# Masking the second attention step by a comparison instead of a match-and-replace pass

## The chip, the cores and the metric

The kernel runs on one core of one Trainium2 chip. The metric is the device time of one launch in microseconds (us). Five engines work side by side, each with its own in-order queue of instructions: TensorE (PE) multiplies matrices and transposes, VectorE (DVE) and ScalarE (ACT) do element-wise work and reductions, GpSimd (POOL) issues the indirect gathers and a few additions, and SyncE (SP) issues most of the plain transfers. On-chip memory is SBUF (128 partitions) and PSUM, where matmul results land; HBM holds the arrays and what is stored in between.

## The reference, cut to what matters

Two graph layers follow each other on 3327 nodes with 256 features. The first has two steps; each builds a 3327 x 3327 attention matrix, keeps in each row the largest probabilities that together reach 90% of the row's mass, and scales the rest of the row to sum 1:

```python
def _top_p_attention(X, W1, W2, W3):
    q = X @ W1.T @ W2.T
    k = X @ W3.T
    probs = softmax(q @ k.T, axis=-1)
    idx = argsort(-probs, axis=-1)
    sp = take_along_axis(probs, idx, axis=-1)
    keep_sorted = cumsum(sp, axis=-1) - sp < 0.9
    mask = zeros(probs.shape, bool).at[rows, idx].set(keep_sorted)
    A = probs * mask
    return A / maximum(A.sum(-1, keepdims=True), 1e-12)

R = row_normalised(adj + I)
for n in range(2):                 # step 0, step 1
    A = _top_p_attention(Xa, W1, W2, W3)
    Xf = R @ Xf
    Xa = A @ Xa
    Z = Z + Xf @ U1[n].T + Xa @ U2[n].T
layer_0 = layernorm(X + Z)         # added to x
# layer 1: relu(D^-1/2 adj D^-1/2 h W.T + b), added to x
```

The sort is stable: of several equal values at the cut only as many are kept as the mass needs.

## The kernel before

The 3327 nodes are tiled into `NB` = 26 blocks of 128 rows. A block of an attention step holds a strip `e` of 128 x 3327 values exp(logit) in SBUF (three such strips, tag "e"). The work has these stages: a start that normalises x and makes keys and queries; step 0 over 26 blocks, mixed with the listing of the sparse adjacency and its gathered products; step 1 over 26 blocks, mixed with the second adjacency product and the layer norms; and a late stage with the second layer (gathered or dense adjacency products, output matmul, store).

**One block of attention** (`attention`, L1321) is a set of named pieces. `lg`/`ex`: PE makes the logits `p_l`, ACT turns them into `e` with a row sum z. `guess`, `ev1r`, `ev1s`, `st1`, in step 1 also `mass`, `tail`, `ev2s`, `btw1`, `sec1`: ACT passes over `e` (written to `ja`, L927) and short 128 x 1 operations on ACT and DVE close in on a threshold t a little above the cut. `win` (L1049): DVE copies the values up to t into a strip `w` of the same size, with their sum. `wm`: 16 MAX8 operations (L1056) take the 8 largest of each of 16 windows of `w`. `sort` (L1060 to L1069): five MAX8 with match-and-replace between them sort out the 40 largest, `val`. `cut` (`window_cut`, L1071): a prefix sum of `val` starts from the mass above t; a value is dropped where its prefix has reached 90% of z (`out_` is then -1e30, otherwise 0), and `kept8` (L1092) receives the eight smallest kept values of each row, the smallest first.

**The mask** differs between the steps. In step 0, a further `cut6` counts ties: `tied` (L1095) is the sum of `out_` over the values of `val` that are at least the smallest kept one, so it is 0 without and at most -1e30 with a dropped value equal to it. `drop` (`drop_rest`, L1111, operation at L1114) then keeps `e >= kept8[0]` and sums the kept into `den`. In step 1, `match` (`mark_kept`, L1105, operation at L1109) first copies `e` to `w` and replaces one entry for each of the eight values of `kept8` by 1e30; `drop` keeps the entries whose `w` is greater than `kept8[0]`. So of equal values only as many are kept as `kept8` lists.

After the mask come the groups of PE transposes `tr` (`p_t`, L1128, two PSUM buffers), ACT copies `atc` (`at`, L1134) and matmuls `att` (`att_acc`, L1143), four blocks of 128 at a time. In step 1, `block_1` (L1436) then makes the residual and norms (`resid`, `input2`), `node2` writes the next layer's input `hn` (ACT, L1284, with a `shift` from DVE, L1283), and `stn` stores it.

**Order.** Nothing is scheduled at run time. `plan_block` (L1473) gives each piece of block i the time BASE + PERIOD * i + SHIFT + place, with the places written out in the table `PLACES`, and `Plan.run` emits the pieces in the order of these times. This order is the order within each engine's queue; `in_steps` (L278) splits a helper at its yields into pieces such as cut0 to cut6.

**The checks.** After the last piece the flags `good` (L1723 to L1741) collect for each row and step whether the 40 values sufficed, whether the cut lies inside them, and whether ties could have gone wrong: for step 0 from `tied`, for step 1 from `kept8[0] < kept8[7]`. One bad row makes the branch at L1746 run `network_bits` (L1663), which computes everything again with a bisection over the bits of the threshold (`nucleus_bits`, L1612: 27 passes over the strip and one more for each of 52 blocks).

Of the kernel before, what the change touches and what calls it, by code (L numbers as in the profile page):

```python
# [10 lines left out]
F32 = mybir.dt.float32  # L11
# [3 lines left out]
ALU = mybir.AluOpType  # L15
AX = mybir.AxisListType

P = 128
N = 3327
NB = (N + P - 1) // P  # L20
# [43 lines left out]
BIG = 1e30  # L64
FILL = 8
# [70 lines left out]
        btw1=-17.852, st14=-15.208, aux0=-14.988, aux1=-14.22, sec10=-12.922, sec11=-12.131, sec12=-10.743,  # L136
        thr=-7.89, sec13=-7.788, nt2=-2.992, win=2.783, wm2=6.046, wm0=6.444, wm1=6.454, wm3=6.526, sort0=8.121,
        sort1=8.162, sort2=9.437, sort3=10.527, sort4=11.217, sort5=12.023, sort6=12.773, sort7=13.564, sort8=15.249,
        cut0=15.328, sort9=15.348, cut1=16.458, cut2=17.341, cut3=18.102, cut4=18.886, cut5=19.961, match=21.123,
        drop=23.999, tr0=28.827, atc0=29.172, tr4=29.605, tr1=32.779, att0=32.801, tr2=32.803, atc1=33.007,  # L140
        att1=33.809, atc4=34.739, tr3=34.759, atc2=36.727, att2=37.933, tr5=38.539, tr6=39.45, atc3=40.18,
        att3=40.29, ldx=44.319, atc5=45.361, atc6=45.991, ldh=48.128, att4=48.571, inv=49.727, att5=50.339,
# [135 lines left out]
def in_steps(do, name, n, work):  # L278
    steps = iter(())

    def step():
        nonlocal steps
        if not started:
            steps = work()
            started.append(True)
        next(steps, None)

    started = []
    do.update((f"{name}{k}", step) for k in range(n))
# [19 lines left out]
def tile_kernel(ctx: ExitStack, tc: tile.TileContext, x, adj_t, w1t, w2t, w3t, u1t, u2t, ln_g, ln_b, wt, bias, out):  # L309
    nc = tc.nc  # L310
    nc.scalar.preload_act_table_set("natural_log_exp_and_others")

    const = ctx.enter_context(tc.tile_pool(name="const", bufs=1))
    res = ctx.enter_context(tc.tile_pool(name="res", bufs=1))
    big = ctx.enter_context(tc.tile_pool(name="big", bufs=1))
    work = ctx.enter_context(tc.tile_pool(name="work", bufs=2))
    small = ctx.enter_context(tc.tile_pool(name="small", bufs=3))
# [92 lines left out]
    kept8 = const.tile([P, 2 * NB, 8], F32, name="kept8")  # L410
# [9 lines left out]
    listed = const.tile([P, NB], F32, name="listed")  # L420
    crowd = const.tile([P, NB], F32, name="crowd")
    edge = const.tile([P, 2 * NB], F32, name="edge")
    tied = const.tile([P, NB], F32, name="tied")
    hidden = const.tile([P, 2 * NB], F32, name="hidden")

    def inv_sqrt(dst, src, eps):
# [375 lines left out]
    def query_load(step, s, i):  # L802
        s["q"] = work.tile([P, P], F32, name="q", bufs=3)
        for half in range(2):
            nc.sync.dma_start(s["q"][half * DA : (half + 1) * DA], q_hbm[step][i * DA : (i + 1) * DA])
# [52 lines left out]
    def logit_group(s, kt, g):  # L858

        c0, w = LOGIT_GROUPS[g]  # L860
        s["l", g] = pl = ps_l.tile([P, 2 * GROUP_W], F32, tag="psl", name="p_l")
        for c in range(0, w, LOGIT_W):
            cw = min(LOGIT_W, w - c)
            for half in range(2):
                rows, at = slice(half * DA, (half + 1) * DA), half * GROUP_W + c
                nc.tensor.matmul(  # L866
                    pl[:, at : at + cw], s["q"][rows, :], kt[rows, c0 + c : c0 + c + cw], start=True, stop=True
                )
# [7 lines left out]
    def exp_group(s, g):  # L876

        c0, w = LOGIT_GROUPS[g]
        if "e" not in s:
            s["e"] = big.tile([P, N + FILL], F32, tag="e", name="e", bufs=3)  # L880
            s["zp"] = z_free[0]
            z_free.append(z_free.pop(0))
        nc.scalar.activation(  # L883
            halves(s["e"])[:, :, c0 : c0 + w], logits_of(s.pop(("l", g)))[:, :, :w], AF.Exp,
            accum_out=s["zp"][:, g : g + 1],
        )

    def col(name):
        return small.tile([P, 1], F32, name=name)
# [39 lines left out]
    def eval_over_by_vector(s):  # L929

        junk = big.tile([P, N + FILL], F32, tag="w", name="w_over")[:, :N]
        s["over"] = col("over")
        ev = s["e"][:, :N]
        nc.vector.scalar_tensor_tensor(
            junk, ev, s["t"], ev, op0=ALU.max, op1=ALU.subtract, accum_out=s["over"]
        )
# [134 lines left out]
    def window_cut(i, step, s):  # L1071


        at, depth = step * NB + i, DEPTH
        s["pre"] = pre = small.tile([P, DEPTH + 1], F32, name="pre", bufs=3)
        nc.vector.tensor_sub(pre[:, 0:1], s["z"], s["below"])
        yield
        val = s.pop("val")
        nc.vector.tensor_tensor_scan(
            pre[:, 1 : depth + 1], val[:, :depth], val[:, :depth], initial=pre[:, 0:1], op0=ALU.add, op1=ALU.bypass  # L1080
        )
        yield
        out_ = small.tile([P, DEPTH], F32, name="out_", bufs=2)
        nc.vector.tensor_scalar(out_[:, :depth], pre[:, :depth], s["thr"], -BIG, op0=ALU.is_ge, op1=ALU.mult)
        yield
        neg = small.tile([P, DEPTH], F32, name="neg", bufs=2)
        nc.vector.tensor_sub(neg[:, :depth], out_[:, :depth], val[:, :depth])
        yield
        neg8 = small.tile([P, 8], F32, name="neg8")
        nc.vector.max(neg8, neg[:, :depth])  # L1090
        yield
        nc.vector.tensor_scalar_mul(kept8[:, at, :], neg8, -1.0)  # L1092
        if step == 0:
            yield
            nc.vector.scalar_tensor_tensor(  # L1095
                out_[:, :depth], val[:, :depth], kept8[:, at, 0:1], out_[:, :depth], op0=ALU.is_ge, op1=ALU.mult,
                accum_out=tied[:, i : i + 1],
            )

    def window_edge(i, step, s):  # L1100

        at = step * NB + i
        nc.vector.tensor_tensor(edge[:, at : at + 1], s.pop("pre")[:, DEPTH - 1 : DEPTH], s["thr"], op=ALU.subtract)

    def mark_kept(i, step, s):  # L1105


        s["w"] = big.tile([P, N + FILL], F32, tag="w", name="w")
        nc.vector.match_replace(s["w"], kept8[:, step * NB + i, :], s["e"], BIG)  # L1109

    def drop_rest(i, step, s):  # L1111
        den, ev = col("den"), s["e"][:, :N]
        kept, op = (ev, ALU.is_ge) if step == 0 else (s.pop("w")[:, :N], ALU.is_gt)
        nc.vector.scalar_tensor_tensor(  # L1114
            ev, kept, kept8[:, step * NB + i, 0:1], ev, op0=op, op1=ALU.mult, accum_out=den
        )
        s["den"] = den

# [202 lines left out]
    def attention(step, i, s, kt, v):  # L1321

        do = {}
        s.update(at={})
        do["ldq"] = lambda: query_load(step, s, i)
        for n in range(NZ):
            do[f"lg{n}"] = lambda n=n: logit_group(s, kt, n)
            do[f"ex{n}"] = lambda n=n: exp_group(s, n)
        in_steps(do, "guess", 7 if step else 9, lambda: first_guess(s, step))
        by_vector = i < BY_VECTOR[step]  # L1330
        do["ev1r"] = lambda: eval_over_by_vector(s) if by_vector else eval_pass(s, AF.Relu, "over")
        do["ev1s"] = lambda: eval_pass(s, AF.Sign, "sign")
        do["thr"] = lambda: set_thr(step, s)
        if step == 0:
            in_steps(do, "st1", 9, lambda: step_0(s))
        else:
            in_steps(do, "mass", 3, lambda: prepare_mass(s))
            do["half"] = lambda: prepare_half(s)
            in_steps(do, "tail", 4, lambda: tail_slope(s))
            in_steps(do, "st1", 5, lambda: step_1(s))  # L1340
            do["aux0"] = lambda: prepare_size(s)
            do["aux1"] = lambda: prepare_num(s)
            do["aux2"] = lambda: prepare_goal(s)
            do["ev2s"] = do["ev1s"]
            do["btw1"] = lambda: count_between(s)
            in_steps(do, "sec1", 4, lambda: secant(s))
            do["nt2"] = lambda: last_t(s)
        do["win"] = lambda: window(s)
        for n in range(4):
            do[f"wm{n}"] = lambda n=n: [window_max(s, k) for k in range(4 * n, 4 * n + 4)]  # L1350
        in_steps(do, "sort", 10, lambda: window_sort(i, step, s))
        in_steps(do, "cut", 6 if step else 7, lambda: window_cut(i, step, s))
        do["edge"] = lambda: window_edge(i, step, s)
        if step == 1:
            do["match"] = lambda: mark_kept(i, step, s)
        do["drop"] = lambda: drop_rest(i, step, s)
        do["inv"] = lambda: invert(s)
        for g in range(GROUPS):
            do[f"tr{g}"] = lambda g=g: attend_turn(s, g)
            do[f"atc{g}"] = lambda g=g: attend_copy(s, g)  # L1360
            do[f"att{g}"] = lambda g=g: attend_sum(s, g, v)
        return do
# [359 lines left out]

    good = small.tile([P, 2 * NB], F32, name="good", bufs=1)  # L1723
    nc.vector.tensor_tensor(good, hidden, kept8[:, :, 0], op=ALU.is_lt)
    also = small.tile([P, 2 * NB], F32, name="also", bufs=1)
    nc.vector.scalar_tensor_tensor(good, edge, 0.0, good, op0=ALU.is_ge, op1=ALU.mult)
    nc.vector.scalar_tensor_tensor(good, kept8[:, :, 0], BIG / 2, good, op0=ALU.is_lt, op1=ALU.mult)
    nc.vector.tensor_tensor(also, kept8[:, :, 0], kept8[:, :, 7], op=ALU.is_lt)
    nc.vector.tensor_scalar(also[:, :NB], tied, -1.0, None, op0=ALU.is_ge)
    nc.vector.tensor_mul(good, good, also)  # L1730
    for c in range(LAST, P):
        for s in range(2):
            g = good[:, (s + 1) * NB - 1 : (s + 1) * NB]
# [54 lines left out]
```

## Time and profile before

| | us |
|---|---|
| three timed runs | 1647.74, 1652.57, 1652.86 |
| their median | 1652.57 |
| the profiled execution | 1856.47 |
| its span, first to last instruction | 1854.7 |
| DVE, PE, ACT, POOL busy in the span | 1301.9, 1543.8, 1139.2, 1004.3 |
| step 0, about | 90 to 930 |
| step 1, about | 965 to 1608 |
| late stage | 1608 to 1855 |

All durations below come from the one profiled execution, which took longer than the timed runs. The page gives busy time by engine, the span in 40 slices of 46.4 us with a digit for tenths of busy time, the groups of instructions by line and operation (busy us, mean ns of one, idle time of the engine just before them and what ended it), and the chain of work that ended last. A row "engine line waited for <- what" sums the idle time of an engine before that line's instructions by what ended it. Matmul ends are modelled and matmuls overlap, so a busy PE isn't a PE at its peak.

### The profile page before, as it was taken

The page shows a single profiled execution, that of the slowest core. Times are in us where ns is not written, and L with a number is a line of the kernel's source. Part 1 is how long each engine was busy: PE and PEld are TensorE (multiplying, and loading weights), DVE is VectorE, ACT ScalarE, POOL GpSimd, SP SyncE. Part 2 cuts the span into 40 slices and gives each one's busy share as a digit, 9 for nine tenths or more (in the row PEclk, how much of TensorE's full clock was granted, in tenths as well). Part 3 has the DMA queues.
Part 4 walks back from the last instruction along what each step waited for, and adds up shares of the span by engine and source line. Part 5 has one row for each costly group of instructions (what it writes and reads, how often), then busy time and mean ns, then how long its engine had stood idle before and what let it go on. Part 6 is the DMA issues. An engine that isn't in the chain of part 4 may idle for free.

```text
span 1854.7 us, 24872 instructions
## 1 busy us (share of the span) xinstructions
PE 1543.8 (83%) x7372; PEld 1191.4 (64%) x7372; DVE 1301.9 (70%) x3965; ACT 1139.2 (61%) x2692; POOL 1004.3 (54%) x808
## 2 busy tenths in 40 slices
PE   5957698878977788787867999999999998968786
PEld 3535476756765566666645777777777777757675
DVE  5596577856865677676629999999999999301111
ACT  3564566645664565666468999999999995100000
POOL 0076465767456456675535665365566461256663
PEclk9968799988988999898987999999999999989998
DMA  6555566645534555453443343333344442647643
GB/s 187 172 170 178 156 178 197 198 133 169 175 120 123 181 147 165 154 172 89 125 145 119 115 121 120 109 116 110 109 118 124 136 120 79 206 142 244 201 142 107
DMA packets 149167, 272.26 MB, mean 147 GB/s; under 512 B 29603, under 2 KB 94496, under 8 KB 148000
## 3 DMA queue, kind: packets, MB, share of 16 engines
q1 hardware_dynamic: 109456, 181.58, 30.2%
q0 software_dynamic: 33536, 87.08, 17.0%
q10 hardware_dynamic: 6032, 1.93, 0.5%
q8 instruction: 60, 0.98, 0.2%
q14 instruction: 83, 0.68, 0.1%
HBM read 221.08 MB, written 49.41 MB: 146 GB/s over the span
## 4 chain that ended last, share of the span: by engine, by line
DVE 22%; PE 13%; issue 11%; another core or an unknown queue 5%; ACT 4%; DMA 1%; POOL 1%; SPq 0%; DVEq 0%; ACTq 0%; POOLq 0%
DVE cand L1056 6%; DVE w L1109 5%; PE att_acc L1143 3%; PE late_acc L702 2%; PE late_sums L1554 2%; ACT ja L927 2%; PE p_t L1128 1%; DVE cand L1069 1%; DVE val L1066 1%; PE adj_acc L702 1%; PE p_o L1299 1%; PE p_l L866 1%; DVE e L1114 1%; DVE bn_st L442 1%
## 5 line engine op out<-in xcount | busy, mean ns | idle before, releaser
L692 POOL DMA_INDIRECT vg<-y_hbm,v_idx x208 | 327.7, 1576 | 273.3 <-PE adj_acc L702 184.1
L678 POOL DMA_INDIRECT ac<-in_adj_t,a_idx x208 | 264.6, 1272 | 253.1 <-DVE own L619 84.7
L1143 PE MATMUL att_acc<-h,at 128*128 128x256 f32 (+1 forms) x1352 | 353.0, 406 | 54.5 <-issue 30.3
L927 ACT ACTIVATE ja<-e,t 128x3327 uint8<-128x3327 f32 x127 | 389.6, 3068 | 0.7
L1134 ACT COPY at<-p_t 128x512 f32<-128x512 f32 (+1 forms) x364 | 197.6, 547 | 238.4 <-remote 123.4
L1143 PEld LDWEIGHTS att_acc<-h,at 128*128 128x128 f32 (+1 forms) x1352 | 266.5, 204 | 111.8 <-issue 43.6
L692 POOL DMA_INDIRECT vg<-gb_hbm,v_idx x208 | 247.6, 1190 | 135.8 <-PE adj_acc L702 72.2
L1143 PE MATMUL att_acc<-xa,at 128*128 128x256 f32 (+1 forms) x1352 | 321.0, 382 | 0.0
L1128 PE MATMUL p_t<-ident,e 128*128 128x128 f32 x1352 | 216.3, 287 | 83.7 <-DVE e L1114 38.3
L1143 PEld LDWEIGHTS att_acc<-xa,at 128*128 128x128 f32 (+1 forms) x1352 | 252.4, 192 | 31.4
L1128 PEld LDWEIGHTS p_t<-ident,e 128*128 128x128 f32 x1352 | 166.7, 147 | 144.3 <-issue 39.4
L1056 DVE MAX8 cand<-w 128x8 f32<-128x208 f32 x832 | 238.6, 360 | 0.2
L702 PE MATMUL adj_acc<-vg,ac 128*128 128x257 f32 (+1 forms) x832 | 229.3, 388 | 2.5 <-issue 1.3
L866 PE MATMUL p_l<-kt,q 64*128 64x512 f32 (+1 forms) x832 | 194.7, 577 | 35.0 <-ACT e L883 27.6
L1049 DVE SCALAR_TENSOR_TENSOR w<-e,t 128x3327 f32<-128x3327 f32 x52 | 191.2, 3676 | 41.5 <-ACT t L897 17.9
L692 POOL DMA_INDIRECT vg<-hn_hbm,v_idx x144 | 136.9, 950 | 97.0 <-PE late_acc L702 48.2
L883 ACT ACTIVATE e<-p_l 128x2048 f32<-128x2048 f32 x104 | 161.6, 1554 | 34.4 <-remote 10.1
L702 PEld LDWEIGHTS adj_acc<-vg,ac 128*128 128x128 f32 x832 | 149.2, 192 | 27.5 <-issue 7.0
L866 PEld LDWEIGHTS p_l<-kt,q 64*128 64x128 f32 x832 | 78.5, 199 | 124.4 <-issue 80.6
L730 ACT COPY xt_k<-p_turn 128x256 f32<-128x256 f32 x52 | 19.0, 370 | 177.9 <-PE late_acc L702 78.6
L570 DVE TENSOR_REDUCE most<-adj_sb 128x7 f32<-128x896 f32 x104 | 105.2, 1012 | 2.0 <-DMA adj_sb<-in_adj_t 1.1
L1114 DVE SCALAR_TENSOR_TENSOR e<-e,kept 128x3327 f32<-128x3327 f32 x26 | 95.7, 3680 | 2.1 <-DVE kept L1092 1.7
(397 smaller groups left out, 2128.6 us busy)
## 6 DMA issues: line engine op xcount, KB each, us to landing
ac<-ac_hbm SPq DMA_DIRECT2D x70, 512.0 KB
adj_sb<-in_adj_t SPq DMA_DIRECT2D x78, 448.0 KB
ac_hbm<-ac SPq DMA_DIRECT2D x26, 512.0 KB
adj_row<-in_adj_t SPq DMA_DIRECT2D x8, 1664.0 KB
adj_sb<-in_adj_t SPq DMA_DIRECT2D x26, 320.0 KB
gb_hbm<-gb SPq DMA_DIRECT2D x26, 256.0 KB
gb<-gb_hbm SPq DMA_DIRECT2D x26, 256.0 KB
q<-q_hbm SPq DMA_DIRECT2D x104, 32.0 KB
```

Of the source, the lines that this page charges most:

```text
L678: nc.gpsimd.indirect_dma_start(s["list"][:, k, :], None, adj_rows, bass.IndirectOffsetOnAxis(ap=s["a_idx"][:, k : k + 1], axis=0))
L692: nc.gpsimd.indirect_dma_start(t[:, :D], None, hbm[:, :], bass.IndirectOffsetOnAxis(ap=v_idx[:, i, k : k + 1], axis=0))
L702: nc.tensor.matmul(s["acc"][:, :width], s["ac"][:, k, :], rows[:, :width], start=(k == 0), stop=(k == SLOTS - 1))
L866: nc.tensor.matmul(pl[:, at : at + cw], s["q"][rows, :], kt[rows, c0 + c : c0 + c + cw], start=True, stop=True)
L883: nc.scalar.activation(halves(s["e"])[:, :, c0 : c0 + w], logits_of(s.pop(("l", g)))[:, :, :w], AF.Exp, accum_out=s["zp"][:, g : g + 1],)
L927: nc.scalar.activation(junk, s["e"][:, :N], f, bias=s["t"], scale=-1.0, accum_out=s[name])
L1049: nc.vector.scalar_tensor_tensor(w[:, :N], ev, s["t"], ev, op0=ALU.is_le, op1=ALU.mult, accum_out=s["below"])
L1056: nc.vector.max(s["cand"][:, 8 * n : 8 * n + 8], s["w"][:, c0 : c0 + cw])
L1114: nc.vector.scalar_tensor_tensor(ev, kept, kept8[:, step * NB + i, 0:1], ev, op0=op, op1=ALU.mult, accum_out=den)
L1128: nc.tensor.transpose(pt[:, c : c + P], s["e"][:, b * P : (b + 1) * P], ident)
L1134: nc.scalar.copy(at[:, :w], pt[:, :w])
L1143: nc.tensor.matmul(s["att"][:, :D], at[:kb, c : c + P], v[b][:kb, :D], start=(b == 0), stop=(b == NB - 1))
```

## The change

Step 1 takes over the mask of step 0. `cut6` runs in both steps and `tied` has a column for each step and block; `mark_kept` goes; `drop_rest` compares `e` itself with `kept8[0]`. The plan of step 1 loses the piece `match` at 21.123 and gains `cut6` at 20.011, right behind `cut5`; all other places stay. The final check uses `tied` for both steps in place of `also`.

```diff
-        cut0=15.328, ... cut5=19.961, match=21.123,
+        cut0=15.328, ... cut5=19.961, cut6=20.011,
...
-    tied = const.tile([P, NB], F32, name="tied")
+    tied = const.tile([P, 2 * NB], F32, name="tied")
...
         nc.vector.tensor_scalar_mul(kept8[:, at, :], neg8, -1.0)
-        if step == 0:
-            yield
-            nc.vector.scalar_tensor_tensor(
-                out_[:, :depth], val[:, :depth], kept8[:, at, 0:1], out_[:, :depth], op0=ALU.is_ge, op1=ALU.mult,
-                accum_out=tied[:, i : i + 1],
-            )
+        yield
+        nc.vector.scalar_tensor_tensor(
+            out_[:, :depth], val[:, :depth], kept8[:, at, 0:1], out_[:, :depth], op0=ALU.is_ge, op1=ALU.mult,
+            accum_out=tied[:, at : at + 1],
+        )
...
-    def mark_kept(i, step, s):
-        s["w"] = big.tile([P, N + FILL], F32, tag="w", name="w")
-        nc.vector.match_replace(s["w"], kept8[:, step * NB + i, :], s["e"], BIG)
...
-        kept, op = (ev, ALU.is_ge) if step == 0 else (s.pop("w")[:, :N], ALU.is_gt)
         nc.vector.scalar_tensor_tensor(
-            ev, kept, kept8[:, step * NB + i, 0:1], ev, op0=op, op1=ALU.mult, accum_out=den
+            ev, ev, kept8[:, step * NB + i, 0:1], ev, op0=ALU.is_ge, op1=ALU.mult, accum_out=den
         )
...
-        in_steps(do, "cut", 6 if step else 7, lambda: window_cut(i, step, s))
+        in_steps(do, "cut", 7, lambda: window_cut(i, step, s))
...
-        if step == 1:
-            do["match"] = lambda: mark_kept(i, step, s)
...
-    also = small.tile([P, 2 * NB], F32, name="also", bufs=1)
...
-    nc.vector.tensor_tensor(also, kept8[:, :, 0], kept8[:, :, 7], op=ALU.is_lt)
-    nc.vector.tensor_scalar(also[:, :NB], tied, -1.0, None, op0=ALU.is_ge)
-    nc.vector.tensor_mul(good, good, also)
+    nc.vector.scalar_tensor_tensor(good, tied, -1.0, good, op0=ALU.is_ge, op1=ALU.mult)
```

More of the change, by code (lines that the diff above doesn't have):

```diff
@@ L138 @@
         sort1=8.162, sort2=9.437, sort3=10.527, sort4=11.217, sort5=12.023, sort6=12.773, sort7=13.564, sort8=15.249,
-        cut0=15.328, sort9=15.348, cut1=16.458, cut2=17.341, cut3=18.102, cut4=18.886, cut5=19.961, match=21.123,
+        cut0=15.328, sort9=15.348, cut1=16.458, cut2=17.341, cut3=18.102, cut4=18.886, cut5=19.961, cut6=20.011,
         drop=23.999, tr0=28.827, atc0=29.172, tr4=29.605, tr1=32.779, att0=32.801, tr2=32.803, atc1=33.007,
```

## The prediction

> **What bounds the kernel now.** I read the page's busy table and its slices first. VectorE (DVE) shows 9 in every slice from the 22nd to the 34th, ScalarE (ACT) and TensorE (PE) are hardly below it there, and this stretch is attention step 1, where the change sits. Next I cut the span into stretches; columns are busy us of PE, PE weight load, DVE, ACT and POOL with instruction counts, then PE clock, DMA share and GB/s:
>
> ```profile
> 90.00:930.00 840.00, 668.40 (x3180) 508.02 (x3181) 600.12 (x1956) 493.66 (x1223) 512.18 (x416) 0.89 0.52 157
> 986.00:1034.00 48.00, 44.49 (x217) 34.52 (x216) 45.54 (x126) 42.68 (x88) 27.42 (x19) 0.93 0.37 114
> 1034.00:1530.00 496.00, 469.90 (x2395) 366.22 (x2394) 491.94 (x1398) 473.74 (x1044) 291.42 (x192) 1.00 0.39 117
> 1530.00:1600.00 70.00, 58.52 (x289) 50.61 (x288) 59.73 (x154) 31.94 (x79) 10.41 (x8) 0.93 0.32 100
> ```
>
> Step 0 (first row) is bound by no single engine. In the third row DVE is busy 491.9 of 496 us (99.2%), ACT 473.7 (95.5%), PE 469.9 (94.7%). So step 1 runs at DVE's pace, but the next two engines are 4 to 5% behind. The match_replace of one block starts at 1033.92 us and the one 21 blocks later at 1532.40, so a block takes 498.5 / 21 = 23.74 us.
>
> Then the groups of the same stretch that the change touches:
>
> ```profile
> L1114 DVE SCALAR_TENSOR_TENSOR e<-w,kept,e 128x3327 f32<-128x3327 f32 x21 | 77.8, 3707 | 0.1
> L1109 DVE MATCH_REPLACE8 w<-kept,e 128x3335 f32<-128x3335 f32 x21 | 76.0, 3617 | 0.0
> L1109 DVE MATCH_VALUE_LOAD w<-kept,e 128x8 f32 x21 | 1.9, 91 | 0.3
> ```
>
> Last, what ACT and PE waited for there (total us, times, longest):
>
> ```profile
> ACT at L1134 <- PE p_t L1128: 5.4, 12, 1.2
> ACT hn_rest L1284 <- DVE shift L1283: 4.6, 11, 0.6
> PE p_t L1128 <- DVE e L1114: 14.9, 20, 2.0
> PE p_t L1128 <- ACT at L1134: 6.0, 20, 0.8
> PE p_l L866 <- ACT e L883: 3.1, 6, 0.6
> ```
>
> ACT lists only 15 us of waits over 21 blocks; PE's largest is for the masked e. These lists decide how much of DVE's gain can be cashed.
>
> [...] eight att_acc matmuls start to start take 1.73 us, 0.216 each, and the next group follows at once, so I treat PE as nearly full. [...]
>
> **The change part by part.**
> Removed, per step-1 block: MATCH_VALUE_LOAD 0.091 + MATCH_REPLACE8 3.617 = 3.71 us of DVE; over 26 blocks 96.4 us.
> Added, per block: the tie count, a SCALAR_TENSOR_TENSOR of 128x40 with an accumulator read. Step 0 already has it: 0.252 + 0.082 us in the trace at L1095; starts overlap by about 0.09 us, so some 0.25 to 0.33, taken as 0.33. It may expose a latency behind kept8, seen as 0.03 to 0.1 us between such dependent ops; bound 0 to 0.1. Sum 26 x 0.33 = 8.7 us.
> Kept: the drop reads e instead of w. In step 0 this form takes 3680 ns, in step 1 the w form 3707: bound -0.04 to 0 us a block; taken as 0. No DMA, PE or ACT instruction changes, no queue is passed, and buffer w is no longer written twice a block (all its users are on DVE, in order, so no wait goes with it). At the end three small ops on the flags (0.38 + 0.14 + 0.21) become one of about 0.2: at most 0.5 us, just ahead of a 26.9 us wait for gathered rows, taken as 0.
> DVE thus falls from 491.9 / 21 = 23.4 to 23.4 - 3.71 + 0.33 = 20.0 us a block. If all of it counted: 3.38 x 26 = 88 us.
>
> But what is late next? ACT: its own gaps in the stretch sum to 22.7 us, 1.08 a block: 6.1 ahead of the at copies (PE's transposes come late because the drop is late), 8.3 ahead of the hn activations (waiting for DVE's shift, queued among other DVE work), and 8.3 between dependent 128x1 ACT ops, which stay. If the first vanishes and the second falls to about half (the trip ACT to DVE and back remains), ACT needs 23.74 - (6.1 + 4.1) / 21 = 23.25; if both go, 23.05. PE: idle 26.2 us in 21 blocks, 14.9 of it on the drop, so 23.74 - 14.9 / 21 = 23.0, at best 22.5. So ACT becomes the bound at about 23.2 us a block, a gain of 0.5, with both ends 0 and 1.1 (ACT without any gap, 22.66). Over 21.6 blocks between the first and the last block of ACT's dense run: 11 us (0 to 24).
>
> The two ends add to this. Start: block 0's chain waits for its match (986.1 to 989.6) with ACT idle behind it 1.6 + 1.0 + 1.4 us; I take 2.5. End: from 1555 on ACT runs out of work and DVE alone carries blocks 24 and 25, so two match steps leave the chain, 7 us for DVE; PE has 18.9 us of block 24 from 1563.9, and stood idle 2.5 and 4.1 us ahead of the two drops, so what passes is 6.6. After that the chain (transposes, the residual's store and reload, hn, gathers, outputs to 1854.7) moves forward whole; nothing there waits on an earlier fixed time.
> Sum: 11 + 2.5 + 6.6 = 20 us. The profiled execution would go from 1856.5 (span 1854.7 plus 1.8) to about 1836. The median 1652.6 lies 204 us lower than the profiled one. The stretch that I argue from is made of back-to-back instructions of fixed length, with few waits on DMA; the waits on DMA and POOL, and clocks below 1, lie in step 0 and the late part, so I carry over the 20 us unchanged: 1632.
>
> **The rivals.**
> *DVE's whole gain arrives.* If ACT and PE lose their overheads outside a profile, up to 88 us: 1565 to 1605. For: DVE at 99%, and its waits are nil. Against: ACT ops are 95% busy by their own durations, and no row shows these shrinking. 12%.
> *Another wait takes its place.* PE waits for ACT's copies (two PSUM buffers for p_t, 6.0 us already) and ACT for PE, so the pace stays 23.7; the end alone passes and is lost at the reload of hz (9.6 us of DMA between 1594.3 and 1603.9): 1648 to 1657. For: both engines stand 5% below DVE, and the order in each queue was laid out for the old work. 9%.
> *Ties call the slow network.* Slower side. The old step 1 marks exactly as many equal values as are kept. The new one keeps every value equal to the smallest kept one, and flags the row if a dropped one of the 40 sorted values equals it; one flagged row of 3327 makes the last branch run network_bits. Its nucleus_bits has 28 passes of 3.76 us and 27 pairs of small ops of about 0.37 a block: 115 us, x 52 blocks = 6,000 us on DVE alone, so over 7,650 us, likelier 9,000. It decides at a single exact tie at a cut. I worked out the values at the cut from the reference and its inputs: in double precision the closest pair in step 1 is 1.8 float spacings apart (step 0: 42), and in twelve float32 evaluations with different orders of summation three had one or two tied rows in step 1, none in step 0. Against: nine had none; the profile can't tell. 19%.
>
> **How the numbers follow.** The likeliest case (60%) is 1632 with its own range 1617 to 1646. With 1565 to 1605 at 12%, 1648 to 1657 at 9% and the slow network at 19%, the range 1575 to 1657 leaves out 19% and the far edge of the second case, about 20%. 0.3% is 5 us, about the spread of the three runs (1647.7 to 1652.9). Faster: 0.60 + 0.12 = 0.72; same 0.09; slower 0.19.
>
> **What would show it.** Right: no MATCH_REPLACE8 of 3335 left, 52 instructions at the tie count, step-1 starts of the window op 23.1 to 23.4 us apart, DVE below 90% and ACT at 97% or more, PE's wait for the masked e mostly gone and DVE now waiting for ACT. The last window op some 20 us earlier, and the part behind it as long as before. Wrong: a pace near 20 us (DVE was the only bound), a pace of 23.7 with new waits between PE and ACT, or a span of many thousand us with over a thousand 3327-wide passes behind the outputs.

## The result, and the profile after

The changed kernel takes 1631.6 us (four executions, 1627.8 to 1635.6), the kernel before 1650.6 beside it: a ratio of 0.9886 with a 95% interval of 0.9855 to 0.9917, so 19 us less (14 to 24). The forecast was 1632, 20 us less. No row was flagged by the tie count: the span ends at 1626 us with no second network behind it.

The kernel before was timed near 1650 us but profiled at 1856, and the changed kernel was profiled at 1628, so before and after are compared in two traces of one set (runs 1 and 2 below, 1847 and 1837 us) or by step 1's own landmarks.

The stretches of the changed kernel, columns as before (busy us of PE, PE weight load, DVE, ACT, POOL with counts, PE clock, DMA share, GB/s); its step 1 begins near 808 us:

```profile
90.00:780.00 690.00, 635.45 (x3257) 498.64 (x3258) 599.67 (x1960) 499.49 (x1237) 550.19 (x416) 0.96 0.63 193
860.00:1350.00 490.00, 471.51 (x2412) 369.22 (x2412) 432.78 (x1420) 475.00 (x1056) 282.91 (x192) 1.00 0.39 118
1350.00:1425.00 75.00, 70.04 (x348) 59.88 (x345) 55.33 (x184) 36.01 (x89) 10.96 (x10) 0.95 0.41 135
```

In the second row DVE is busy 432.8 of 490 us, 88.3% where it was 99.2%; ACT now leads with 96.9%, PE follows with 96.2%. The waits of the same stretch (total us, times, longest), first DVE's, then ACT's, then PE's; those of ACT and PE in the kernel before stand in the prediction:

```profile
DVE tail_d L976 <- ACT mass L897: 42.0, 21, 3.0
DVE prop L1159 <- PE adj_acc L702: 6.4, 11, 1.3
...
ACT hn_rest L1276 <- DVE shift L1275: 3.2, 11, 0.6
ACT kt L1276 <- DVE shift L1275: 1.8, 6, 0.5
...
ACT at L1126 <- PE p_t L1120: 0.3, 1, 0.3
...
PE p_t L1120 <- ACT at L1126: 14.1, 24, 1.6
PE p_l L866 <- ACT e L883: 3.1, 7, 0.6
```

In the kernel before, DVE's largest wait was this one (run 1, over 466 us):

```profile
DVE tail_d L976 <- ACT mass L897: 0.8, 1, 0.8
```

The reader sees the bound change hands: DVE, which hardly waited, now waits 2.0 us in each block for ACT's `mass`; PE no longer waits for the masked e, but for ACT's copies; ACT's wait for PE's transposes ahead of these copies has gone from 5.4 to 0.3 us. The chain of work that ended last in this stretch, as shares by line, says the same ("issue" is time in which the engine waited for nothing that the profile shows). First of the kernel before, then of the changed one; both rows go on:

```profile
by line: issue 29.5%; DVE cand L1056 18.0%; DVE w L1109 14.8%; DVE cand L1069 4.6%; DVE val L1066 4.2%; DVE bn_st L442 2.7%; DVE x_in L1275 2.0%; DVE hz L1273 1.6%; DVE hz L1258 1.5%; DVE hz_r L1242 1.5%; DVE hz_r L1247 1.3%; DVE prop L1167
```

```profile
by line: ACT ja L927 35.9%; ACT e L883 11.0%; ACT at L1126 9.5%; PE att_acc L1135 5.8%; issue 2.4%; ACT t L897 2.0%; PE p_l L866 2.0%; PE p_t L1120 1.7%; ACT u L897 1.7%; ACT bn_rr L430 1.5%; ACT ln L429 1.5%; ACT mass L897 1.4%; ACT ln_v L
```

Of the removed operation (L1109 before) no row is left, and the mask in the new form costs what the old did (3707 ns before):

```profile
L1106 DVE SCALAR_TENSOR_TENSOR e<-e,kept 128x3327 f32<-128x3327 f32 x21 | 77.8, 3705 | 0.0
```

Pace below means the mean distance of window operations (`w<-e,t`) from the fourth to the twenty-third block of step 1: 23.20 us in the changed kernel. "Step 1" means from the start of the first window operation to the start of the last `hn` activation.

### The profile page after: what moved, and what is told of

Its sections match the earlier page's. It is cut to its first block, busy times and chain, and to the rows that moved or that the text cites. A ratio compares the mean times of both kernels' runs of the same rounds, so it can differ in the third digit from the quotient of the medians.

```text
span 1626.0 us, 24877 instructions
## 1 busy us (share of the span) xinstructions
PE 1479.3 (91%) x7372; PEld 1157.9 (71%) x7372; DVE 1219.6 (75%) x3963; ACT 1135.5 (70%) x2692; POOL 1033.8 (64%) x808
## 3 DMA queue, kind: packets, MB, share of 16 engines
q10 hardware_dynamic: 6032, 1.93, 0.5%
## 4 chain that ended last, share of the span: by engine, by line
PE 41%; ACT 31%; DVE 10%; DMA 5%; issue 5%; POOL 4%; SPq 0%; DVEq 0%; POOLq 0%; ACTq 0%
PE att_acc L1135 15%; ACT ja L927 13%; PE late_sums L1544 5%; PE adj_acc L702 5%; ACT e L883 5%; PE p_t L1120 4%; PE p_l L866 4%; ACT at L1126 4%; PE late_acc L702 3%; POOL ac L678 2%; DVE cand L1056 2%; DVE e L1106 2%; DMA vg<-hn_hbm,v_idx 1%; DMA vg<-gb_hbm,v_idx 1%; PE p_o L1291 1%
## 5 line engine op out<-in xcount | busy, mean ns | idle before, releaser
L692 POOL DMA_INDIRECT vg<-y_hbm,v_idx x208 | 319.2, 1535 | 242.4 <-PE adj_acc L702 180.9
L678 POOL DMA_INDIRECT ac<-in_adj_t,a_idx x208 | 285.1, 1371 | 147.1 <-DVE own L619 84.0
L1135 PE MATMUL att_acc<-h,at 128*128 128x256 f32 (+1 forms) x1352 | 324.8, 387 | 0.0
L692 POOL DMA_INDIRECT vg<-gb_hbm,v_idx x208 | 265.1, 1275 | 63.5 <-issue 40.9
L1135 PEld LDWEIGHTS att_acc<-h,at 128*128 128x128 f32 (+1 forms) x1352 | 253.5, 193 | 41.4 <-issue 7.6
L1120 PE MATMUL p_t<-ident,e 128*128 128x128 f32 x1352 | 209.0, 280 | 34.7 <-ACT at L1126 21.6
L1120 PEld LDWEIGHTS p_t<-ident,e 128*128 128x128 f32 x1352 | 162.8, 143 | 91.2 <-ACT at L1126 33.4
L866 PE MATMUL p_l<-kt,q 64*128 64x512 f32 (+1 forms) x832 | 181.9, 553 | 31.2 <-ACT e L883 28.7
L1049 DVE SCALAR_TENSOR_TENSOR w<-e,t 128x3327 f32<-128x3327 f32 x52 | 191.2, 3676 | 22.5 <-ACT t L897 22.5
L1106 DVE SCALAR_TENSOR_TENSOR e<-e,kept 128x3327 f32<-128x3327 f32 x52 | 191.9, 3691 | 0.5
L866 PEld LDWEIGHTS p_l<-kt,q 64*128 64x128 f32 x832 | 74.7, 191 | 113.2 <-issue 66.2
```

The costliest lines, as they stand in the source:

```text
L678: nc.gpsimd.indirect_dma_start(s["list"][:, k, :], None, adj_rows, bass.IndirectOffsetOnAxis(ap=s["a_idx"][:, k : k + 1], axis=0))
L692: nc.gpsimd.indirect_dma_start(t[:, :D], None, hbm[:, :], bass.IndirectOffsetOnAxis(ap=v_idx[:, i, k : k + 1], axis=0))
L866: nc.tensor.matmul(pl[:, at : at + cw], s["q"][rows, :], kt[rows, c0 + c : c0 + c + cw], start=True, stop=True)
L1049: nc.vector.scalar_tensor_tensor(w[:, :N], ev, s["t"], ev, op0=ALU.is_le, op1=ALU.mult, accum_out=s["below"])
L1106: nc.vector.scalar_tensor_tensor(ev, ev, kept8[:, step * NB + i, 0:1], ev, op0=ALU.is_ge, op1=ALU.mult, accum_out=den)
L1120: nc.tensor.transpose(pt[:, c : c + P], s["e"][:, b * P : (b + 1) * P], ident)
```

## The experiments

The question was which of three theories holds: ACT sets the pace from now on, at about 23.2 us a block, with PE just behind (the prediction); DVE still sets it and each microsecond of DVE counts; or PE sets it.

### 1 and 2: before and changed kernel in one set

No edit.

> The kernel before, profiled once more, to have its trace beside the changed one's. The profiled execution of before took 1856 us against a median of 1652. If the extra 204 us lay outside step 1, as the prediction took for granted, this trace has step 1's pace at 23.7 us a block again, DVE at 99% there, and its span is nearer 1650, with the difference in step 0 and the late part. If step 1 had been stretched too, its pace is well below 23.7.

> The changed kernel, timed in more rounds: 19 to 21 us less than before. If the first result was luck within the spread of runs, anything from 10 to 30.

The changed kernel: 0.9895 (0.9859 to 0.9932) of before, 19 us less (13 to 26) than 1855. The stretches of the two traces, before first:

```profile
90.00:930.00 840.00, 673.40 (x3220) 513.97 (x3221) 601.26 (x1959) 497.07 (x1233) 508.84 (x416) 0.88 0.52 158
1034.00:1500.00 466.00, 441.27 (x2243) 344.78 (x2242) 461.04 (x1329) 444.63 (x990) 263.36 (x177) 1.00 0.39 117
```

```profile
90.00:930.00 840.00, 671.16 (x3186) 510.26 (x3187) 600.76 (x1955) 493.90 (x1228) 513.49 (x416) 0.88 0.51 157
1038.00:1500.00 462.00, 444.34 (x2272) 348.22 (x2272) 408.93 (x1339) 448.19 (x996) 262.89 (x179) 1.00 0.39 119
```

The first expectation was wrong in its span: 1844.8 us, not near 1650. It was right in what it was for, that the extra time lies outside step 1: step 1 of the changed kernel takes 615.4 us in its first trace (span 1626.0 us), 615.6 here (span 1835.0), and 613.9 in a third (run 12). The difference between the first two lies in front (first window at 808.6 against 972.1 us) and behind (202 against 247 us), where PE's clock in the records is 0.96 to 0.98 in the shorter trace and 0.88 to 0.90 in the longer.

Step 1 shrinks from 634.2 to 615.6 us, by 18.6, which is the measured gain within its interval. By landmarks: from the first window to the fourth 1.3 us less, over the 21 blocks to the twenty-fifth 13.1, from there to the last hn 4.2. The pace falls from 23.73 to 23.19. These shares are those of one pair of traces: with the first profile of before in place of run 1 they are 3.7, 12.3 and 4.1 us.

### 3: only the first and the last two blocks

```diff
+ENDS = (0, 24, 25)
+def compares(i, step):
+    return step == 0 or i in ENDS
...
-        kept, op = (ev, ALU.is_ge) if step == 0 else (s.pop("w")[:, :N], ALU.is_gt)
+        kept, op = (ev, ALU.is_ge) if compares(i, step) else (s.pop("w")[:, :N], ALU.is_gt)
...
-        if step == 1:
+        if not compares(i, step):
             do["match"] = lambda: mark_kept(i, step, s)
```

> The kernel before, with the comparison (and the tie count, its flag left out for step 1) in blocks 0, 24 and 25 of step 1 alone; blocks 1 to 23 keep match_replace. Theory (steady part 11, start 2.5, end 6.6): 9 us less than before, so about 11 short of the changed kernel. Rival, DVE alone sets the time and every block counts alike: 20 x 3 / 26 = 2.3 us less. Rival, the whole gain is the ends: 20 less.

0.9959 (0.9937 to 0.998): 7.6 us less (3.7 to 11.7). Three blocks of 26 bring more than their 2.3 us, and far from all 19. In its trace step 1 takes 629.9 us, 4.3 less than before: 0.5 at the start, 4.6 at the end, and the pace between is 23.77. The expected 9 is inside the interval of the time; the trace, with 4.3 us, says that it was too much, above all at the start.

### 4: the tie count taken away

```diff
-        yield
-        nc.vector.scalar_tensor_tensor(out_[:, :depth], ..., accum_out=tied[:, at : at + 1])
+        if step == 0:
+            yield
+            nc.vector.scalar_tensor_tensor(out_[:, :depth], ..., accum_out=tied[:, at : at + 1])
```

> The changed kernel without the tie count of step 1 (26 small DVE operations and step 1's part of the tie flag left out). Theory, DVE has some 2 us to spare in each block: 0 to 1 us less than the changed kernel. Rival, DVE still sets the pace: 26 x 0.33 = 8.7 us less.

0.9907 (0.9872 to 0.9942), beside 0.9895 with the count; pace 23.22, step 1 again 615.6 us. The times alone would not separate 0 from 8.7 us; the two step-1 lengths, equal to 0.1 us, do (three traces of the changed kernel itself lie between 613.9 and 615.6): the count is free.

### 5 to 7: a filler on each engine in turn

Into each step-1 block of the changed kernel went one more operation, whose output nobody reads: on DVE half a window pass where the match stood, on ACT 900 columns behind the sign pass, on PE four transposes made twice. Of each edit the operation alone is shown.

```diff
+        nc.vector.scalar_tensor_tensor(
+            w[:, :1664], s["e"][:, :1664], s["t"], s["e"][:, :1664], op0=ALU.is_le, op1=ALU.mult)
```

```diff
+        nc.scalar.activation(junk[:, :900], s["e"][:, :900], AF.Relu, bias=s["t"], scale=-1.0)
```

```diff
-        for b in range(4 * g, min(4 * g + 4, NB)):
+        again = s.get("step") == 1 and g == 2
+        for b in list(range(4 * g, min(4 * g + 4, NB))) * (2 if again else 1):
```

> The changed kernel with one more DVE operation in each block of step 1, where the match stood: half a window pass (1664 wide, some 1.9 us) whose output nobody reads. Theory, DVE waits 2 us or more in each block for ACT: the pace stays near 23.2 us a block, 0 to 5 us more than the changed kernel, from the two ends. Rival, DVE sets the pace: 26 x 1.9 = 49 us more.

> The changed kernel with one more ACT operation in each block of step 1, right behind the first sign pass: 900 columns of e, some 0.95 us start to start, output unread. Theory, ACT sets the pace with its own gaps only: pace 24.1 us a block, 20 to 25 us more than the changed kernel. Rival, PE sets the pace and ACT has 0.5 us or more to spare: 0 to 12 us more.

> The changed kernel with the third group's four transposes made twice in each block of step 1 (0.66 us of PE, same values). Theory, PE still has some 0.9 us idle in a block: 0 to 6 us more than the changed kernel, part of it in the end where PE alone works (2 x 0.66). Rival, PE sets the pace: 0.66 x 26 = 17 us more.

| | ratio to before (95%) | pace | step 1 |
|---|---|---|---|
| changed (first set) | 0.9886 (0.9855 to 0.9917) | 23.20 | 615.4 |
| + DVE filler | 0.9897 (0.9882 to 0.9913) | 23.22 | 616.8 |
| + ACT filler | 1.0071 (1.0055 to 1.0086) | 24.41 | 643.8 |
| + PE filler | 0.9922 (0.9906 to 0.9937) | 23.42 | 621.8 |

The changed kernel was not run again in the fillers' set; the kernel before took 1650.5 us there and 1650.6 in the first set, so the ratios are compared across the two.

The DVE filler costs 1 to 2 us in all instead of 49. Its own trace shows what paid for it: the wait that stood at 42 us (over 490 us) in the changed kernel has shrunk to 13 (over 464 us).

```profile
876.00:1340.00 464.00, 446.23 (x2282) 349.60 (x2281) 445.67 (x1359) 449.74 (x1000) 290.35 (x180) 1.00 0.40 119
...
DVE tail_d L976 <- ACT mass L897: 13.1, 17, 1.3
```

DVE is busy 96% of the stretch and the pace stays at 23.22: an operation of 1.95 us in most blocks (1.93 to 2.40 in its trace), about half as long as the removed match, is hidden behind ACT. The ACT filler counts fully:

```profile
L1106 ACT ACTIVATE ja<-e,t 128x900 uint8<-128x900 f32 x20 | 20.9, 1045 | 0.6
```

1.05 us of work raises the pace by 1.21, step 1 by 28 us and the time by some 30, above the expected 20 to 25: the operation was taken as 0.95, and 26 blocks at 1.05 are 27. Where the other 0.16 us a block go was not followed. PE's filler passes about half. The expected 0.66 us equals the listed length of a group of four transposes behind a wait (at 1566.78 in run 2); by its distance to what follows a group of four takes 0.44 us (1550.32 to 1550.76 there), so 0.22 of 0.44 us a block arrive, and 6 us in all (5.9 from the two ratios, 6.4 in step 1), at the upper edge of the expected 0 to 6. So added work on ACT arrives in full, and PE stands less than a microsecond behind it.

### 8 and 9: less work on ACT

Five short operations move from ACT to DVE (first pair of lines as an example); then, in a second kernel, `rd` and `shift` also move ahead in the plan. In both, two short pieces (`half`, `aux2`) also get slightly other places; this is left out below, and the notes behind `#` are not in the kernels.

```diff
-        scale = fma("rd", t["n"]["rr"], d_inv[:, i : i + 1], 0.0)
+        scale = col("rd")
+        nc.vector.tensor_mul(scale, t["n"]["rr"], d_inv[:, i : i + 1])
...
-        kc = fma("kc", s["c"], 2.0 * PSEUDO, 0.0)           # likewise thr, uh, goal
```

```diff
-        do["node2"] = lambda: node_2(i, s, hn[i])
+        do["shift"] = lambda: node_2(i, s)                  # rd and shift on DVE
+        do["node2"] = lambda: node_2_end(s, hn[i])          # the activation on ACT
...
+        shift=84.2, node2=90.831,
```

> The changed kernel with five short step-1 operations (thr, uh, kc, goal, rd) moved from ACT to DVE, about 0.9 us of ACT a block, and rd's move also takes away ACT's round trip to DVE ahead of hn (0.3 us a block). Theory: ACT falls from 23.2 to about 22.0 us a block, PE (22.3 busy) becomes the bound, pace 22.5 to 22.8, 10 to 16 us less than the changed kernel. Rival, PE already sets the pace: 0 to 3 us less.

> The kernel with less ACT work, and in it DVE's rd and shift moved ahead: right behind the masking pass two blocks later instead of behind the tail operations that wait for ACT's mass. Theory, the missing gain went into ACT's wait for this shift (14 us over 20 blocks): with shift early ACT stands at 22.0 us a block or a little above, pace 22.6 to 22.9, 7 to 13 us less than the changed kernel. Rival, PE and its two buffers of transposes hold the pace at 23.2 whatever ACT does: 0 to 3 us less.

The first: 0.9868 (0.9847 to 0.9889), pace 23.17, step 1 614.7. A miss: 10 to 16 us were expected, and it can't be told from the changed kernel. ACT's busy time fell by 9.5 us over 20 blocks, from the first row below to the second. That is 0.5 us a block where 0.9 were expected, and ACT's waits rose:

```profile
875.00:1340.00 465.00, 447.23 (x2290) 350.41 (x2288) 411.27 (x1346) 450.46 (x1001) 266.30 (x182) 1.00 0.39 119
875.00:1340.00 465.00, 448.13 (x2290) 349.38 (x2287) 419.74 (x1441) 440.93 (x904) 246.44 (x181) 1.00 0.39 119
```

Its main waits for `shift` in this stretch:

```profile
ACT hn_rest L1284 <- DVE shift L1283: 7.3, 11, 1.1
ACT kt L1284 <- DVE shift L1283: 2.9, 5, 0.9
...
ACT hn_adj L1284 <- DVE shift L1283: 1.0, 1, 1.0
```

The shift stands in DVE's queue behind `tail_d`, which waits for ACT's mass (in one block of this trace `tail_d` starts at 1085.16 after a wait of 1.64 us, and `shift` at 1086.00); ACT, no longer computing rd in between, reaches hn sooner and waits there instead. These waits for `shift` sum to 11.9 us in the stretch, against 6.6 in the changed kernel. The second kernel takes this wait away: none for the shift is left in its list. Pace 23.00, step 1 608.9 us against 613.9 in the changed kernel of its own set; 0.9865 (0.9831 to 0.99) against that kernel's 0.9887. So the new wait was part of the lost gain, but only about 0.2 us a block came back of the 0.3 to 0.6 expected, and the times can't be told apart. ACT's busy time a block fell from 22.5 us in run 12 to 22.1, so of the relief less than half arrives: by this run ACT led the next limit by some 0.2 us a block. Between PE and ACT, the largest waits left are PE's for ACT's copies and ACT's for PE's transposes; these are two of the rows (1060 to 1480 us):

```profile
ACT at L1133 <- PE p_t L1127: 2.1, 7, 0.5
...
PE p_t L1127 <- ACT at L1133: 9.8, 15, 1.3
```

That PE's two buffers of transposes then hold the pace at 23.0 is only argued; a third buffer was not tried.

### 10: less work on PE

```diff
+        less = s.get("step") == 1 and g == 2
-        for b in range(4 * g, min(4 * g + 4, NB)):
+        for b in range(4 * g, 4 * g + 2 if less else min(4 * g + 4, NB)):
```

> The changed kernel with two of the 26 att blocks of each step-1 block left out (4 matmul instructions, 0.87 us of PE; the attention sum lacks 256 of the nodes). Theory, ACT sets the pace of 23.2: 0 to 6 us less than the changed kernel, 1.7 of it from the end where PE works alone. Rival, PE sets it: 0.87 x 26 = 23 us less.

Pace 23.24, step 1 614.8 against 613.9: with four matmuls less for PE in each block (0.87 us by their distance, 0.216 us each: eight start 1.73 us ahead of what follows, 1550.76 to 1552.49 in run 2; its busy time falls from 403.2 to 391.2 us over 420) nothing is faster. PE's wait for ACT's copies rises over 420 us, from run 12, which is the changed kernel in the same set, to this run:

```profile
PE p_t L1120 <- ACT at L1126: 8.0, 13, 1.6
PE p_t L1120 <- ACT at L1126: 21.3, 27, 2.1
```

The time's ratio, 0.9846 (0.9798 to 0.9893), overlaps the changed kernel's 0.9887 (0.9853 to 0.9921) and is not read further. PE alone does not set the pace.

### 11: the price of the slow network

```diff
-    nc.vector.tensor_scalar(lost, lost, -1.0, 1.0, op0=ALU.mult, op1=ALU.add)
+    nc.vector.tensor_scalar(lost, lost, -1.0, 2.0, op0=ALU.mult, op1=ALU.add)
```

> The changed kernel with the count of lost rows made at least 1 in each partition, so that the slow network always runs behind the fast one. The prediction's price: more than 6000 us on top (52 blocks x 115 us of DVE), likelier 7400, so 7600 to 9500 us in all. If the passes were shared out over engines or overlapped, less.

9817 us in its one execution, where the changed kernel took 1847: 7970 us on top, more than half of it in one row, 26 of the bisection's passes for each of 52 blocks:

```profile
L1610 DVE SCALAR_TENSOR_TENSOR w<-e,cand_b 128x3327 f32<-128x3327 f32 x1352 | 4979.1, 3683 | 45.5
```

This lies above the expected 7600 to 9500, and would also do so from the forecast's 1632 us (9602). What comes on top, put at 7400, is 8% more.

### 12: the changed kernel in the third set

> The changed kernel beside the others of this set, for the comparison on one chip: 18 to 20 us less than before.

0.9887 (0.9853 to 0.9921), 21 us less (15 to 27) than 1868; pace 23.20, step 1 613.9.

## Why the prediction was right

The sum came out at 20 us and 19 were measured. Term by term:

- **DVE's load.** 3.71 us a block removed, 0.33 added. Runs 4 and 5 show that neither the added count nor 1.95 us more moves the pace (23.22 in both): after the change DVE waits 2.0 us in each block. Had DVE stayed the bound (the first rival, 88 us), run 5 would have cost 49. That rival fell. The mask, a SCALAR_TENSOR_TENSOR that also sums, took 3.68 us in step 0 and 3.71 us in step 1 before, and takes 3.71 us in step 1 after: unchanged, as the prediction took it.
- **The new bound.** ACT at "about 23.2 us a block": measured 23.20, and 1.05 us put on ACT raised it by 1.21. Its working has one half wrong: the wait for transposes did vanish (6.1 to 0.3 us), but the wait for the shift fell only from 8.3 to 6.6, not to half. In the trace this shift stands behind DVE's new wait for ACT in the same queue (in one block `tail_d` waits 1.88 us to 1082.35, and `shift` starts at 1083.02); in run 8 ACT's waits for the shift were 11.9 us, and with the shift moved ahead (run 9) none was listed. ACT leads by little: 0.5 us less of its work a block brought 0.2 in run 9. One reading was slightly off: ACT's listed waits before sum to 14.0 us, not 15.
- **The sizes.** Blocks between the ends: 11 forecast, 13.1 measured in runs 1 and 2. Start: 2.5 forecast, 1.3 measured. End: 6.6 forecast, 4.2 measured. Over the other pairs of traces on record these are 12.1 to 13.1, 1.3 to 3.7 and 4.1 to 6.1 us. So the blocks between were put too low and the end too high, and the start can't be judged; the errors cancel, and the good total is partly luck. At the end the working took it that PE's idle time ahead of the last two masks would all be saved. This is how PE stood there in run 1 (waits in brackets):

```profile
1555.36 1.94 PE L1128 MATMUL p_t<-ident,e 128*128 128x128 f32 x8 [3.53 <-DVE e L1114]
1578.78 2.58 PE L1128 MATMUL p_t<-ident,e 128*128 128x128 f32 x12 [3.24 <-DVE e L1114]
```

  And these are all of PE's rows with a wait from 1543 us on in run 2:

```profile
1547.19 1.13 PE L1224 MATMUL adj_acc<-u,xt_q 128*128 128x256 f32 x4 [0.65 <-DVE hz_r L1234]
1565.47 1.06 PE L1120 MATMUL p_t<-ident,e 128*128 128x128 f32 x8 [0.49 <-DVE e L1106]
1566.78 0.66 PE L1120 MATMUL p_t<-ident,e 128*128 128x128 f32 x4 [0.24 <-ACT at L1126]
1567.67 0.70 PE L1135 MATMUL att_acc<-xa,at 128*128 128x256 f32 x2 [0.24 <-DVE hz L1250]
```

  Of 6.8 us of PE's waits, 1.6 are still there, in part at other places. Otherwise PE runs without a listed gap to the end of step 1, so the last blocks go at PE's own length, and DVE in turn waits 2.2 us for PE's adj_acc ahead of `prop`. Why 4.2 us and not 5.2 arrive was not followed further.
- **PE "nearly full".** Right as an order (PE next behind ACT). In the changed step 1 PE is listed busy 96.2%, its weight loads 75% (369.2 of 490 us). The filler decides how much room that leaves: 0.44 us more of PE, 2% of a block, was already felt by half (run 7). But PE alone does not set the pace (run 10).
- **The rival of another wait** (pace stays at 23.7, the end lost at the reload of hz) fell: the pace is 23.2, and DVE's wait for that reload is 11.6 us in the first profile of before and 11.4 in run 2. But the kind of wait that it named, between PE and ACT, is what remains between these two at 23.0 when ACT is relieved (9.8 and 2.1 us over 420 in run 9).
- **The slow network.** No row was flagged, so the mechanism was not seen at work on these inputs. Its price, given as 6000 on DVE alone and likelier 7400 in all, is 7970 (run 11). That it stayed away says nothing of other inputs.
- **Carrying 20 us over from a profile 204 us longer than the median.** Right, and shown: step 1 takes 615.4 and 615.6 us in two traces of the changed kernel that are 209 us apart. The reason given was not exact: the prediction's own rows show a clock of 0.93 also at both ends of step 1.

## What to carry to other kernels

Taking work from an engine that was busy 99% paid here only down to the next engine: 3.4 us a block came off by the listed lengths (3.71 less 0.33) and 0.54 arrived. Before counting the rest, add up each other engine's gaps in that stretch and ask which of them the saving closes, and then check with a filler on each engine who sets the pace. The filler showed that ACT is at the bound (1.05 us of work, 1.21 of pace); only taking work away showed by how much it leads, some 0.2 us. Relief that moves an operation to another engine's queue must also be placed: behind an instruction that waits, as `rd` was in run 8, it brought the wait along (ACT's waits for `shift` went from 6.6 to 11.9 us).

## What was not expected of the hardware

The kernel before took 1651 us in one set of experiments (on chip 5) and 1855 and 1868 in the two others (on chips 15 and 9). Step 1 of the changed kernel takes 613.9 to 615.6 us in all three traces of it, so the 200 us lie in step 0 and the late part, where the records show a lower PE clock in the longer traces (0.88 to 0.90 against 0.96 to 0.98). Whether the difference goes with the chip, and whether the clock or the transfers come first, was not studied.

A 128x40 operation on DVE, the tie count, takes 0.26 us in 20 of the 26 step-1 blocks of the changed kernel's first trace, 0.32 in one and 0.67 to 1.22 in five; DVE had room for it. Each of the five overlaps with POOL's addition `x_in<-x_in,bet` (L1260, 0.74 to 0.76 us), and none of the 20 does. In run 12 four take 0.68 to 0.71 us, one 0.32 and the others 0.26. No run moved that addition, so that it is the cause is not shown.
